# Turning the token rows of 100 expert slots: PE transposes and a PSUM copy, or pieces loaded by partition group and one VectorE transpose

## The chip, the cores and the metric

The program runs on one core of a Trainium2 chip. The core has a matmul engine (TensorE, here PE, with its weight loads listed apart as PEld), a vector engine (DVE), a scalar engine (ACT), GpSimd (POOL) and a sync engine (SP) that does no arithmetic here and issues most DMAs. Sixteen DMA engines move data between the chip's memory (HBM) and the on-chip memory (SBUF, 128 partitions). Matmul results land in PSUM. All engines run their own instruction lists in order and wait for each other through semaphores. The metric is the device time of one execution in microseconds, as the median of several.

## What is computed

Four layers are applied to 2,048 tokens of 256 channels (`x` is 2 x 1,024 x 256, all in f32). Each layer conditions the tokens, sends the result through an expert layer and adds it to `x`. Only layers 2 and 3 matter here:

```python
# layer 2, conditioning: 8 experts, two of them per token, gelu
for e in range(N_EXPERTS):
    h = jax.nn.gelu(x_flat @ r_w1[e].T, approximate=False)
    routed_out = routed_out + h @ r_w2[e].T * gates_full[:, e:e + 1]
out = (shared_out + routed_out) / (N_SHARED + TOP_K)
# layer 2, FFN: 8 experts of width 1024, two of them per token, silu-gated
g = jax.nn.silu(jnp.einsum('td,edf->etf', flat, w1_e))
u = jnp.einsum('td,edf->etf', flat, w3_e)
out_e = jnp.einsum('etf,efd->etd', g * u, w2_e)
routed = jnp.einsum('te,etd->td', gates, out_e).reshape(b, s, d)
# layer 3, conditioning: as in layer 2, with other weights
h = jax.nn.gelu(jnp.einsum('nc,ech->enh', xf, W1e), approximate=False)
y = jnp.einsum('enh,ehc->enc', h, W2e)
routed = jnp.einsum('ne,enc->nc', combine, y)
```

Beside the routed experts each of these has shared experts that all tokens pass through. Layer 3's own FFN works on another path (the class `Last`) that the change does not touch.

## The kernel before

**Slots.** Each token goes to two of eight experts. The kernel sorts these 4,096 pairs by expert into slots of 128 rows. POOL scatters each token's row into `xbuf`, an array in HBM with rows of `DR` = 258 numbers: the 256 channels, the token's row number in the result, and the token's expert. The 258 numbers are 1,032 bytes. A slot belongs to one expert, and its 128 rows are multiplied with that expert's weights. In this run layer 2's conditioning ("layer 2's MoE" below) has 35 slots, layer 2's FFN 33, and layer 3's conditioning ("layer 3's MoE") 37. Two of the FFN's 33 slots hold rows of several experts.

**One slot, step by step.** `Slots.fetch` (L1881) lets SP load the slot's 128 rows into `xs`, one row per partition, with all 258 numbers (the issue has line L418). A matmul needs the channels on the partitions, so `Slots.rows` (L1889) turns the rows: `_channel_major` (L495) does two PE transposes of 128x128 into a PSUM tile `ps_cm` (L500), and DVE copies the tile to `xsT` (L1895). Two small DVE operations (L1899, L1902) then compute `sdst`, for each row the row of `tbuf` that its result goes to; rows that do not belong to the slot get a number out of range. In the MoEs, `_gelu_products` (L1970) multiplies `xsT` with the first weight matrix (`cph`, L1976), ACT applies gelu (L1979), PE multiplies with the second matrix (`cpo`, L1983), and DVE copies the result to `ys` (L1985). In the FFN, `_ffn_products` (L1991) does this with two first matrices (`fpg`, `fpu`, L2000), a product on DVE (L2005) and ACT's copy to `ys` (L2012). `Slots.put` (L1907) lets POOL scatter `ys` to `tbuf` by `sdst` (L402).

**Order on PE.** `Series` (L1915) writes PE's order out. A call of `slot` for slot i first asks for the rows of slot i+2 (`fetch`), then puts in the transposes of slot i+1 (`turn`), the first products of slot i, the second products of slot i-1 (`close`), and so on. `stage` chains every group behind the last one with `_behind`, an order without a wait.

**Order on SP.** SP issues the row loads and, from `_expert_load` (L1857), the weight loads of each slot, in one list. A weight load is skipped on the chip when the slot's weight buffers already hold the expert. The MoEs have four sets of weight buffers, the FFN two, and later three. A weight load waits until the slot that used its set before is done. `xs` has four buffers; a row load waits until the small DVE operations of the slot four before are done. The first weights of each stage are issued before the rows. The row loads of a stage wait until all its scatters into `xbuf` have landed.

**Weight layout.** A first matrix of 256 input channels lies in SBUF as 128 partitions x 2 halves (`c`): channel `c * 128 + p` on partition `p`. A row of `xsT` holds the same channels. Each row of a MoE's matrix is 1,024 bytes, of the FFN's first two matrices 4,096.

**After the slots.** `Tokens` loads each token's two results from `tbuf` into tiles `yt` (five buffers of 128x512) and adds them up while PE does the last quarter of the shared experts.

Of the kernel before, what the change touches and what calls it, by code (L numbers as in the profile page):

```python
# [20 lines left out]
P = 128  # L21
D = 256
# [19 lines left out]
class Ring:  # L42


    def __init__(self, t, n):
        self.t, self.n, self.i, self.held = t, n, 0, set()
# [445 lines left out]
    return ps.rearrange("p c d -> p (c d)")  # L492


def _channel_major(k, psum, rows, ref=None, made=None):  # L495


    ps = psum.tile([P, 2, P], F32, name="ps_cm", tag="t", bufs=2)
    for c in range(2):
        i = k.nc.tensor.transpose(ps[:, c, :], rows[:, c * P:(c + 1) * P], k.ident)  # L500
# [24 lines left out]
def _layer0(k):  # L525
# [37 lines left out]
    with ExitStack() as ctx:  # L563
# [92 lines left out]
        shared(1, lambda f, mul, mm: rows_of(4 + f, mm))  # L656
        _layer1_loads0(k, k.pre)
        ahead(-2)
        slots = Slots(k, pool, psum, ref=sent[-1])
# [4 lines left out]
        for i in range(NS):  # L664
            if i < 18 and i % 2 == 1:
                next(mask)
            lo, cols = i * T, []
            while lo < (i + 1) * T:

                e = lo // C  # L670
                n = 64 if i % 3 == 1 else 32
                cols.append((slice(lo - i * T, lo - i * T + n), ws[e]))
                lo += n
            muls.append(split.slot(i, cols))
            next(pre, None)

            ahead(3 * (i * T // C), slots.load)
# [16 lines left out]
    def slots_over():  # L694
        k.yrows = (NS + NOV) * T
        zero = pool.tile([P, 1, DR], F32, name="l0_zero", bufs=1)
        nc.vector.memset(zero[:, :, 0:D], 0.0)
        nc.vector.memset(zero[:, :, D:], NONE)
        _zero_rows(k, ybuf[NS * T:(NS + NOV) * T, :], zero[:, :, 0:D])
        read = k.x.read  # L700
        k.x.read = k.x.read + k.x.new + [_zero_rows(k, xbuf[NS * T:, :], zero).ins.name]
        k.x.begin()
        for t in range(NT):
            k.x.scatter(k.Hr[:, t, :], rows[:, t:t + 1])
        k.ring.held = set(held)
        slots = Slots(k, pool, psum)
# [12 lines left out]
        more(0)  # L719
        k.x.read = read + k.x.read  # L720
        k.ring.i, k.ring.held = free[0], set(free[1])
# [1135 lines left out]
def _expert_load(k, eid, i, to, E, always=False):  # L1857

    nc = k.nc

    e = nc.sync.value_load(eid[0:1, i:i + 1], min_val=0, max_val=E)
    new = {} if always else {"cond": e < E}
    e = nc.s_assert_within(e, 0, E - 1, skip_runtime_bounds_check_because="at E the load is skipped")
    for t, a in to:
        nc.sync.dma_start(t, a[bass.ds(e, 1)].rearrange("o (c p) f -> p (o c) f", p=P), **new)
    return [t for t, _ in to]


# [4 lines left out]
class Slots:  # L1873

    def __init__(self, k, pool, psum, of=None, base=0, ref=None):
        self.k, self.pool, self.psum, self.of, self.base, self.ref = k, pool, psum, of, base, ref
        self.xs, self.dst = {}, {}

    def fetch(self, i):  # L1881

        if i not in self.xs:
            self.xs[i] = self.pool.tile([P, DR], F32, name="xs", bufs=4)
            self.load = self.k.x.load(self.xs[i], self.k.xbuf[i * P:(i + 1) * P, :])
            if self.ref is not None:
                _behind(self.k, self.load, self.ref)

    def rows(self, i, made=None):  # L1889
# [5 lines left out]
        turned = nc.vector.tensor_copy(xT, _channel_major(k, self.psum, xs, made=made))  # L1895
        if self.of is not None:

            n = pool.tile([P, 1], F32, name="sn", bufs=3)
            j = nc.vector.tensor_tensor(n, xs[:, D + 1:D + 2], self.of[:, i:i + 1], ALU.not_equal)  # L1899
            _behind(k, j, turned)  # L1900
            self.dst[i] = pool.tile([P, 1], U32, name="sdst", bufs=5)
            j = nc.vector.scalar_tensor_tensor(self.dst[i], xs[:, D:D + 1], -float(self.base), n,  # L1902
                                               ALU.add, ALU.add)
            _behind(k, j, turned)
        return xT

    def put(self, i, y):  # L1907
        if self.of is None:
            self.k.nc.scalar.dma_start(self.k.ybuf[i * P:(i + 1) * P, :], y)
        else:  # L1910

            self.k.t.scatter(y, self.dst.pop(i), bounds_check=2 * N - 1, oob_is_err=False)


class Series:  # L1915
# [1 line left out]

    def __init__(self, k, slots, ids):  # L1920
        self.k, self.slots, self.ids = k, slots, list(ids)
        self.xT, self.last, self.old, self.soon = {}, None, None, False
        self.fetch(0)
        self.fetch(1)
        self.turn(0)

    def stage(self, insts):

        for i in insts:
            if self.last is not None:  # L1930
                _behind(self.k, i, self.last)
        self.last = insts[-1]

    def fetch(self, n):
        if n < len(self.ids):
# [8 lines left out]
    def slot(self, i, products, weights, soon=False):  # L1944

        n = self.ids.index(i)
        self.fetch(n + 2)
        self.turn(n + 1)
        if self.soon:
            self.close()  # L1950
        self.soon = soon
        p = products(self.xT.pop(i), *weights())
        self.stage(next(p))
        self.close()
        part = next(p)
# [106 lines left out]
class Split:  # L2062
# [9 lines left out]
    def stage(self, insts):  # L2072

        for i in insts:
            if self.last is not None:
                _behind(self.k, i, self.last)
        self.last = insts[-1]

    def product(self, name, xT, cols, j):
        ps = self.psum.tile([P, self.F], F32, name=name, tag="mm")  # L2080
# [58 lines left out]
def _cond_moe(k, name, wr, bias, W1, W3, W2, nf, hold, R1, R2, gate_mult, final, lead, most, next=None):  # L2139
# [73 lines left out]
    by = Slots(k, pool, psum, of, base)  # L2213

    def slots(lo, hi):
        series = Series(k, by, range(lo, hi))
        for i in range(lo, hi):
            series.slot(i, _gelu_products(k, pool, psum), lambda: _slot_weights(k, eid, i, sets, E))
        series.close()
# [41 lines left out]
def _layer2_ffn(k):  # L2261
# [65 lines left out]
        return [_expert_load(k, mid, 3 * m + q, sets[j], E) for q, j in enumerate(to) if j is not None]  # L2327

    def slots(ids):
        series = Series(k, by, ids)  # L2330
        for n, i in enumerate(ids):
            if i == NS:
                series.slot(i, _mixed_products(k, pool, psum), lambda: mixed(0, 0, 1, 2), True)
# [562 lines left out]
```

## Time and profile before

| | |
|---|---|
| median of 8 runs | 1399.71 us (1397.0 to 1404.9) |
| profiled execution | 1401.7 us, its span 1400.0 us |
| layer 2's MoE, 438 to 511 us | PE busy 69.43 of 73.00 us, DMA share 0.67 |
| layer 2's FFN, 687 to 1035 us | PE busy 345.30 of 348.00 us, DMA share 0.55 |
| layer 3's MoE, 1162.5 to 1243 us | PE busy 75.80 of 80.50 us, DMA share 0.70 |
| PE transposes of slot rows, all layers | 258 of 273 ns (24 slots of layer 0 and the 105 of layers 2 and 3) |
| DVE copies of the turned rows | 129 of 416 ns |
| row loads issued by SP | 129 of 344 ns each, 129 KB |

How to read it: "busy" is the time in which an engine runs an instruction; matmuls overlap in PE's pipeline, so their lengths add up to more than their cost, and PE's price of an instruction is read from the start of the next. The DMA share is the mean busy share of the sixteen DMA engines. "Released by" or an arrow names what an engine waited for last. Lines of the form L1895 are lines of the kernel before.

### The profile page before, as it was taken

Reading aid. Unit: us, or ns where it says so; the run is one execution under the profiler, and the core shown is the slowest. Engines: PE = TensorE matmul, PEld = TensorE weight load, DVE = VectorE, ACT = ScalarE, POOL = GpSimd, SP = SyncE. Lnnn points to the kernel's source line nnn. Section 1 sums busy time; section 2 is a strip of 40 time slices with the busy share of each in tenths; the row PEclk is TensorE's granted clock in tenths of the full one; section 3 lists DMA queues with packets and bytes.
Section 4 is the critical chain, followed back from the end, with each engine's and each line's share of the span. In section 5 each row is a group of like instructions: output and inputs, shape, how many; then the busy total and the mean of one; then the engine's idle time right before and its main releaser. Section 6 shows DMA issues by size and latency. Waiting matters only on the chain. (4 is left out here: it accounts for less than half of the span.)

```text
span 1400.0 us, 23093 instructions
## 1 busy us (share of the span) xinstructions
PE 1360.0 (97%) x8428; PEld 955.1 (68%) x8431; DVE 460.9 (33%) x1519; ACT 302.1 (22%) x636; POOL 272.6 (19%) x308
## 2 busy tenths in 40 slices
PE   9999999999999999999999999999999999998897
PEld 4644444655657876555599999999975557875685
DVE  4523322325413444511211111111215423458432
ACT  4222221234112122211111111111112212127122
POOL 0400001300432430053000100000000073430441
PEclk9999999999999999999999999999999999999999
DMA  9979992943312852092285456266448247748670
GB/s 312 313 242 347 357 367 88 300 91 136 113 53 86 252 186 79 0 332 70 77 319 168 148 201 218 81 206 222 150 162 288 93 165 243 228 149 282 212 226 16
DMA packets 185424, 265.26 MB, mean 189 GB/s; under 512 B 16759, under 2 KB 134655, under 8 KB 185296
## 3 DMA queue, kind: packets, MB, share of 16 engines
q1 hardware_dynamic: 163984, 221.65, 48.6%
q0 software_dynamic: 13744, 36.63, 7.4%
q10 hardware_dynamic: 7568, 5.34, 1.2%
q8 instruction: 71, 1.16, 0.3%
q14 instruction: 57, 0.47, 0.1%
HBM read 283.67 MB, written 46.82 MB: 236 GB/s over the span
## 5 line engine op out<-in xcount | busy, mean ns | idle before, releaser
L402 POOL DMA_INDIRECT tbuf<-ys,sdst x105 | 103.3, 984 | 462.6 <-ACT ys L2012 301.0
L1675 PE MATMUL spo<-ring,sa 128*128 128x256 f32 x704 | 165.0, 380 | 0.6 <-DVE sa L1703 0.4
L1675 PEld LDWEIGHTS spo<-ring,sa 128*128 128x128 f32 x704 | 132.7, 190 | 46.1 <-issue 28.7
L1703 DVE TENSOR_TENSOR sa<-ssg,spu 128x512 f32<-128x512 f32 x88 | 60.3, 686 | 240.5 <-PE spu L1690 231.2
L2005 DVE TENSOR_TENSOR fa<-fsg,fpu 128x512 f32<-128x512 f32 x62 | 42.6, 687 | 278.4 <-PE fpu L2000 278.4
L2000 PE MATMUL fpg<-xsT,ring 128*128 128x128 f32 x992 | 121.1, 276 | 1.1 <-DMA ring<-in_L_w 1.1
L2000 PE MATMUL fpu<-xsT,ring 128*128 128x128 f32 x992 | 121.0, 275 | 0.6 <-DMA ring<-in_L_w 0.6
L2000 PEld LDWEIGHTS fpg<-xsT,ring 128*128 128x128 f32 x992 | 117.9, 192 | 3.6 <-issue 2.1
L2000 PEld LDWEIGHTS fpu<-xsT,ring 128*128 128x128 f32 x992 | 115.8, 192 | 0.7 <-issue 0.7
L2009 PE MATMUL fpo<-ring,fa 128*128 128x256 f32 x496 | 112.4, 380 | 0.1
L1699 ACT ACTIVATE ssg<-spg 128x512 f32<-128x512 f32 x88 | 52.5, 597 | 267.0 <-PE spg L1690 262.8
L2009 PEld LDWEIGHTS fpo<-ring,fa 128*128 128x128 f32 x496 | 92.0, 191 | 12.2 <-issue 1.1
L1690 PE MATMUL spg<-HT,ring 128*128 128x512 f32 x192 | 92.0, 594 | 3.4 <-issue 2.1
L1690 PE MATMUL spu<-HT,ring 128*128 128x512 f32 x192 | 90.2, 593 | 0.0
L1976 PE MATMUL cph<-xsT,ring 128*128 128x128 f32 x576 | 77.8, 278 | 8.2 <-DMA ring<-in_L_r 5.5
L1976 PEld LDWEIGHTS cph<-xsT,ring 128*128 128x128 f32 x576 | 70.1, 192 | 11.8 <-DVE sn L1899 5.3
L1690 PE MATMUL spg<-XT,ring 128*128 128x512 f32 x160 | 75.6, 594 | 1.2 <-PEq L2223 1.0
L1690 PE MATMUL spu<-XT,ring 128*128 128x512 f32 x160 | 75.4, 592 | 0.0
L1983 PE MATMUL cpo<-ring,ch 128*128 128x256 f32 x288 | 73.8, 380 | 0.0
L2004 ACT ACTIVATE fsg<-fpg 128x512 f32<-128x512 f32 x62 | 37.0, 597 | 143.9 <-PE fpg L2000 143.9
L1690 PEld LDWEIGHTS spu<-HT,ring 128*128 128x128 f32 x192 | 36.2, 190 | 43.9 <-issue 43.7
L1895 DVE COPY xsT<-ps_cm 128x256 f32<-128x256 f32 x129 | 53.8, 418 | 30.9 <-PE ps_cm L500 30.9
(677 smaller groups left out, 1761.5 us busy)
## 6 DMA issues: line engine op xcount, KB each, us to landing
ring<-in_L_w SPq DMA_DIRECT2D x105, 1024.0 KB
ring<-in_L_r SPq DMA_DIRECT2D x72, 512.0 KB
ring<-in_L_r SPq DMA_DIRECT2D x144, 256.0 KB
xs<-xbuf SPq DMA_DIRECT2D x129, 129.0 KB
ring<-in_L_W SPq DMA_DIRECT2D x32, 512.0 KB
yt<-tbuf SPq DMA_DIRECT2D x48, 256.0 KB
XT<-in_L_r SPq DMA_DIRECT2D x16, 512.0 KB
HT<-in_L_r SPq DMA_DIRECT2D x8, 512.0 KB
```

Of the source, the lines that this page charges most:

```text
L402: i = k.nc.gpsimd.indirect_dma_start(out=self.ap, out_offset=bass.IndirectOffsetOnAxis(ap=idx, axis=0), in_=rows, in_offset=None, **end)
L1675: mm = nc.tensor.matmul(po[g // 2][:, g % 2, :], a[:, g * P:(g + 1) * P], W2[:, f, :], start=f == 0 and g % 2 == 0, stop=f == nf - 1, skip ...
L1690: mm = nc.tensor.matmul(ps, W[:, c, f * P:(f + 1) * P], X[:, c, cols], start=c == 0, stop=c == 1)
L1699: k.silu = nc.scalar.activation(sg, pg, AF.Silu)
L1703: mul = nc.vector.tensor_mul(a, sg, pu)
L1895: turned = nc.vector.tensor_copy(xT, _channel_major(k, self.psum, xs, made=made))
L1976: made = [nc.tensor.matmul(ph[:, f, :], R1[:, c, f * P:(f + 1) * P], xT[:, c, :], start=c == 0, stop=c == 1) for f in range(2) for c in ra ...
L1983: made = [nc.tensor.matmul(po, h[:, f, :], R2[:, f, :], start=f == 0, stop=f == 1) for f in range(2)]
L2000: made = [nc.tensor.matmul(ps[:, j, :], W[:, c, (f0 + j) * P:(f0 + j + 1) * P], xT[:, c, :], start=c == 0, stop=c == 1) for ps, W in ((pg, ...
L2004: nc.scalar.activation(sg, pg, AF.Silu)
L2005: nc.vector.tensor_mul(a[:, f0:f0 + 4, :], sg, pu)
L2009: made = [nc.tensor.matmul(po, a[:, f, :], W2[:, f, :], start=f == 0, stop=f == 4 * nh - 1) for f in range(4 * nh)]
```

## The change

It concerns the slots of layers 2 and 3 (`blocks=True`); layer 0's slots are still turned by PE, but their row loads leave out the two last numbers.

- Rows are loaded in four DMAs, one for each group of 32 partitions. Partition 32q + s of the tile `xq` gets, for each block b of 32 rows, the channels 64q to 64q + 63 of row 32b + s, a run of 256 bytes. Two slots that follow each other are loaded by the same four DMAs (`plan`, at most two). The tiles share the five buffers of `yt`.
- One DVE transpose per slot (`StreamTranspose` in the instruction list) turns all 32x32 blocks. Partition 32q + r then holds the channels 64q + 2r and 64q + 2r + 1, that is channels 2p and 2p + 1 on partition p.
- The weights follow: all matrices of a slot but the last are loaded with two neighbouring rows on one partition, so that a partition's part is one run in HBM.
- The first two slots of each MoE and the first of the FFN are still loaded as whole rows and turned by PE, with every second column in each transpose.
- The row numbers and experts of all slots of a stage come in one DMA of 8-byte pieces (`numbers`), and two DVE operations compute all of `sdst` at once. They are called in the first slot after the turn of the second.
- `Series.slot` asks for the rows of slot i+3 as well.

In the instruction lists, PE has 100 pairs of transposes less in the slots that this run executes. SP's list in a MoE is: two whole-row loads, four DMAs of `xq`, the numbers, eight DMAs of `xq`, then by turns the weights of two slots and four DMAs of `xq`. On DVE the first of the two operations on the numbers (a wait for their DMA) stands after the copies of the first two turns and ahead of the third slot's transpose.

```diff
-def _channel_major(k, psum, rows, ref=None, made=None):
+def _channel_major(k, psum, rows, ref=None, made=None, pairs=False):
     ps = psum.tile([P, 2, P], F32, name="ps_cm", tag="t", bufs=2)
     for c in range(2):
-        i = k.nc.tensor.transpose(ps[:, c, :], rows[:, c * P:(c + 1) * P], k.ident)
+        i = k.nc.tensor.transpose(ps[:, c, :], rows[:, c::2] if pairs else rows[:, c * P:(c + 1) * P], k.ident)
...
-    for t, a in to:
-        nc.sync.dma_start(t, a[bass.ds(e, 1)].rearrange("o (c p) f -> p (o c) f", p=P), **new)
+    for n, (t, a) in enumerate(to):
+        form = "o (p c) f -> p (o c) f" if n + 1 < len(to) else "o (c p) f -> p (o c) f"
+        nc.sync.dma_start(t, a[bass.ds(e, 1)].rearrange(form, p=P), **new)
...
+    def plan(self, ids, rows, most):
+        ids = list(ids)
+        while ids:
+            n = 1
+            if ids[0] in rows or not self.blocks:
+                self.group[ids[0]] = None
+            else:
+                while n < most and ids[n:n + 1] == [ids[0] + n]:
+                    n += 1
+                for j in range(n):
+                    self.group[ids[j]] = ids[0], n
+            ids = ids[n:]
...
     def fetch(self, i):
-        if i not in self.xs:
-            self.xs[i] = self.pool.tile([P, DR], F32, name="xs", bufs=4)
-            self.load = self.k.x.load(self.xs[i], self.k.xbuf[i * P:(i + 1) * P, :])
...
+        if group is None:
+            self.xs[i] = self.pool.tile([P, D], F32, name="xs", bufs=4)
+            self.load(self.xs[i], k.xbuf[i * P:(i + 1) * P, 0:D])
+            return
+        lo, n = group
+        if self.of is None:
+            t = self.pool.tile([P, n, 4, 64], F32, name="xq", tag="xs", bufs=4)
+        else:
+            t = self.pool.tile([P, 2, 4, 64], F32, name="xq", tag="yt", bufs=5)
+        for q in range(4):
+            self.load(t[32 * q:32 * q + 32, 0:n].rearrange("p g b k -> p (g b) k"),
+                      k.xbuf[lo * P:(lo + n) * P, 64 * q:64 * q + 64].rearrange("(b s) k -> s b k", s=32))
...
-        turned = nc.vector.tensor_copy(xT, _channel_major(k, self.psum, xs, made=made))
-        if self.of is not None:
-            n = pool.tile([P, 1], F32, name="sn", bufs=3)
-            j = nc.vector.tensor_tensor(n, xs[:, D + 1:D + 2], self.of[:, i:i + 1], ALU.not_equal)
...
+        if self.group[i] is None:
+            self.turned = nc.vector.tensor_copy(xT, _channel_major(k, self.psum, xs, made=made, pairs=self.blocks))
+        else:
+            self.turned = nc.vector.transpose(xT.rearrange("p c (b s) -> p c b s", b=4),
+                                              xs.rearrange("p b (r c) -> p c b r", c=2))
         return xT
+
+    def numbers(self):
+        k, nc, n = self.k, self.k.nc, self.of.shape[1]
+        m = self.pool.tile([P, n, 2], F32, name="xm", tag="xs", bufs=4)
+        k.x.load(m, k.xbuf[0:n * P, D:].rearrange("(i p) d -> p i d", p=P))
+        i = nc.vector.tensor_tensor(m[:, :, 1], m[:, :, 1], self.of, ALU.not_equal)
+        _behind(k, i, self.turned)
+        self.dst = k.rp.tile([P, n], U32, name="sdst", tag="sdst")
+        nc.vector.scalar_tensor_tensor(self.dst, m[:, :, 0], -float(self.base), m[:, :, 1], ALU.add, ALU.add)
...
         self.fetch(n + 2)
         self.turn(n + 1)
+        if self.slots.of is not None and self.slots.dst is None:
+            self.slots.numbers()
...
         p = products(self.xT.pop(i), *weights())
+        self.fetch(n + 3)
...
-        series = Series(k, by, range(lo, hi))
+        series = Series(k, by, range(lo, hi), 0 if lo else 2)
...
-        series = Series(k, by, ids)
+        series = Series(k, by, ids, 1 if ids[0] == NS else 0)
```

More of the change, by code (lines that the diff above doesn't have):

```diff
@@ L658, in _layer0 @@
         ahead(-2)
-        slots = Slots(k, pool, psum, ref=sent[-1])
+        slots = Slots(k, pool, psum, ref=sent[-1], blocks=False)
+        slots.plan(range(NS), (0, 1), 1)
         split = Split(k, pool, psum, slots, F, NS)
@@ L675, in _layer0 @@
             next(pre, None)
-            ahead(3 * (i * T // C), slots.load)
+            ahead(3 * (i * T // C), slots.loaded)
         with k.tc.issue_after(split.up.ins):
@@ L705, in slots_over @@
         k.ring.held = set(held)
-        slots = Slots(k, pool, psum)
+        slots = Slots(k, pool, psum, blocks=False)
         n = nc.values_load(nov[0:1, 0:1], min_val=0, max_val=NOV)
@@ L1873, with __init__, load, rows @@
 class Slots:
-    def __init__(self, k, pool, psum, of=None, base=0, ref=None):
+    def __init__(self, k, pool, psum, of=None, base=0, ref=None, blocks=True):
         self.k, self.pool, self.psum, self.of, self.base, self.ref = k, pool, psum, of, base, ref
-        self.xs, self.dst = {}, {}
-    def fetch(self, i):
-        if i not in self.xs:
-            self.xs[i] = self.pool.tile([P, DR], F32, name="xs", bufs=4)
-            self.load = self.k.x.load(self.xs[i], self.k.xbuf[i * P:(i + 1) * P, :])
-            if self.ref is not None:
-                _behind(self.k, self.load, self.ref)
-    def rows(self, i, made=None):
+        self.xs, self.group, self.dst, self.blocks = {}, {}, None, blocks
+    def plan(self, ids, rows, most):
[10 more added lines that the diff above has]
+            ids = ids[n:]
+    def load(self, t, src):
+        self.loaded = self.k.x.load(t, src)
+        if self.ref is not None:
+            _behind(self.k, self.loaded, self.ref)
+    def fetch(self, i):
+        if i in self.xs:
+            return
+        k, group = self.k, self.group[i]
+        if group is None:
+            self.xs[i] = self.pool.tile([P, D], F32, name="xs", bufs=4)
+            self.load(self.xs[i], k.xbuf[i * P:(i + 1) * P, 0:D])
+            return
+        lo, n = group
[6 more added lines that the diff above has]
+                      k.xbuf[lo * P:(lo + n) * P, 64 * q:64 * q + 64].rearrange("(b s) k -> s b k", s=32))
+        for j in range(n):
+            self.xs[lo + j] = t[:, j]
+    def rows(self, i, made):
         k, nc, pool = self.k, self.k.nc, self.pool
@@ L1894, in rows @@
         xT = pool.tile([P, 2, P], F32, name="xsT", bufs=3)
-        turned = nc.vector.tensor_copy(xT, _channel_major(k, self.psum, xs, made=made))
-        if self.of is not None:
-            n = pool.tile([P, 1], F32, name="sn", bufs=3)
-            j = nc.vector.tensor_tensor(n, xs[:, D + 1:D + 2], self.of[:, i:i + 1], ALU.not_equal)
[L1900 to L1904, printed above, removed]
-        return xT
+        if self.group[i] is None:
[3 more added lines that the diff above has]
+                                              xs.rearrange("p b (r c) -> p c b r", c=2))
+        return xT
+    def numbers(self):
[6 more added lines that the diff above has]
+        nc.vector.scalar_tensor_tensor(self.dst, m[:, :, 0], -float(self.base), m[:, :, 1], ALU.add, ALU.add)
     def put(self, i, y):
@@ L1910, in put, with __init__ @@
         else:
-            self.k.t.scatter(y, self.dst.pop(i), bounds_check=2 * N - 1, oob_is_err=False)
+            self.k.t.scatter(y, self.dst[:, i:i + 1], bounds_check=2 * N - 1, oob_is_err=False)
 class Series:
-    def __init__(self, k, slots, ids):
+    def __init__(self, k, slots, ids, rows=0):
         self.k, self.slots, self.ids = k, slots, list(ids)
         self.xT, self.last, self.old, self.soon = {}, None, None, False
+        slots.plan(ids, self.ids[:rows], 1 if slots.of is None else 2)
         self.fetch(0)
@@ L1931, in stage @@
                 _behind(self.k, i, self.last)
-        self.last = insts[-1]
+        self.last = (insts or [self.last])[-1]
     def fetch(self, n):
@@ L2076, in stage @@
                 _behind(self.k, i, self.last)
-        self.last = insts[-1]
+        self.last = (insts or [self.last])[-1]
     def product(self, name, xT, cols, j):
```

## The prediction

> **What bounds the kernel now.** I read the page's engine totals first, then the instructions that touch the two tiles of a turn (`ps_cm`, `xsT`), then the timeline of one slot, the table by stage, and last the timeline of SP.
>
> ```profile
> span 1400.0 us, 23093 instructions
> PE 1360.0 (97%) x8428; PEld 955.1 (68%) x8431; DVE 460.9 (33%) x1519; ACT 302.1 (22%) x636; POOL 272.6 (19%) x308
> ...
> L500 PE MATMUL ps_cm<-ident,xs x258: 272/273/331, 78.4 to 1238.7; 128*128 128x128 f32 x129
> L1895 DVE COPY xsT<-ps_cm x129: 412/416/425, 78.9 to 1239.2; 128x256 f32<-128x256 f32 x129
> ```
>
> PE is busy nearly all the time, so what PE no longer does can count. But 273 ns is the pipelined length of one transpose, not its price. The price stands in the order of time, here in layer 2's FFN (matmul starts, then lengths):
>
> ```profile
> 806.61 0.38 PE L500 MATMUL ps_cm<-ident,xs 128*128 128x128 f32 x2
> 806.83 1.95 PE L2000 MATMUL fpg<-xsT,ring 128*128 128x128 f32 x16
> ```
>
> Both transposes move the next matmul by 806.83 - 806.61 = 0.22 us. The same 0.22 us stands in the small slots (443.98 to 444.19, 445.95 to 446.17). A small slot is 445.95 - 443.98 = 1.97 us of PE.
>
> The table by stage (span, PE busy, weight loads, DVE, ACT, POOL, clock, DMA share, GB/s) shows where PE is not the only limit. 438 to 511 are the 35 slots of layer 2's MoE, 687 to 1035 the 33 of its FFN, 1162.5 to 1243 the 37 of layer 3's MoE:
>
> ```profile
> 460.00:475.00 15.00, 14.33 (x101) 12.89 (x100) 7.38 (x29) 2.68 (x7) 6.88 (x7) 1.00 0.92 290
> 725.00:800.00 75.00, 75.00 (x572) 72.25 (x571) 13.01 (x35) 10.96 (x21) 6.88 (x7) 1.00 0.53 179
> 1170.00:1185.00 15.00, 13.80 (x93) 12.02 (x92) 6.70 (x26) 2.61 (x7) 6.36 (x7) 1.00 0.98 312
> 1200.00:1215.00 15.00, 12.76 (x87) 11.07 (x85) 6.32 (x25) 2.30 (x6) 5.90 (x6) 1.00 1.00 329
> 1215.00:1230.00 15.00, 15.00 (x109) 13.94 (x108) 8.18 (x32) 2.68 (x7) 7.26 (x8) 1.00 0.51 143
> ```
>
> In the FFN, PE is full and the DMA engines half idle. In the MoEs there are stretches at 0.92 to 1.00 DMA share in which PE loses 0.7 to 2.2 us of 15: the slots that bring new expert weights. In the issue times of SP the weight DMAs that are skipped last 73 ns and the real ones 372 ns, so the two kinds can be counted: of the 31 weight pairs issued between the slots of layer 2's MoE 14 are real, of the 33 in layer 3's 17.
>
> In such a stretch SP has no time left either:
>
> ```profile
> 461.31 0.41 SPq L418 DMA_DIRECT2D xs<-xbuf  x1
> 462.04 1.14 SPq L1865 DMA_DIRECT2D ring<-in_L_r  x2
> 463.28 0.41 SPq L418 DMA_DIRECT2D xs<-xbuf  x1
> 464.01 1.14 SPq L1865 DMA_DIRECT2D ring<-in_L_r  x2
> 465.25 0.41 SPq L418 DMA_DIRECT2D xs<-xbuf  x1
> ```
>
> One row load and two weight loads take SP 463.28 - 461.31 = 1.97 us, the same as PE's slot.
>
> **The change, part by part.**
>
> *PE's turns go.* The lists of instructions show 100 of the 105 slots of layers 2 and 3 without transposes (33 + 32 + 35). At 0.22 us that is 22.0 us of PE, the upper end of what the change can bring.
>
> *DVE turns instead.* The copy from PSUM (416 ns) and two one-column operations (149 to 220 ns and 159 ns) become one transpose of 128x256 f32. No row of this trace is a DVE transpose. From below: the cheapest DVE row, 0.15 us. From above: the 128x512 f32 product, 0.69 us, if it walks its input twice. I take the 128x256 copies, 0.42 us, the same count of elements per partition. In a small slot DVE then does 0.42 + 0.43 (the copy to `ys`) = 0.85 of about 1.76 us, so up to 1.3 us per turn it is hidden by PE; the cover is gone above that. Matmuls no longer wait for a PSUM round trip but for the rows' DMA directly. Rows are issued up to three slots ahead, one more than before, so this costs nothing.
>
> The Trainium skill, "VectorE: DVE Perf Modes", The three transpose paths, gives 311 ns for a 128x128 bf16 transpose on VectorE, in 32x32 blocks only, and 390 ns on TensorE. By these, two halves would make 0.62 us, which is still hidden, so the sum would not move.
>
> *Rows in 256-byte pieces.* The trace also keeps every DMA packet's size and time. Medians: 8 B 9 ns, 256 B 18 ns, 512 B 32 ns, 1,024 B 46 ns, 1,032 B 47 ns, 2,048 B 84 ns. A slot's rows were 128 packets of 1,032 B, 8 on each of 16 engines: 0.38 us. They become 512 packets of 256 B, 32 on each: 0.58 us at 18 ns. The 128 packets of that size were contiguous ones, so 18 ns is the low end; the 512 B price (32 ns, 1.02 us) is the high end. I take 18 ns, the row of the same size. The first weight matrix goes from 256 rows of 1,024 B to 128 of 2,048 B: 16 x 46 = 0.74 us to 8 x 84 = 0.67 us. A slot with new weights thus costs 0.20 - 0.07 = 0.13 us more of all engines.
>
> The Trainium skill, "DMA: Bandwidth & Descriptors", Specifications, speaks against this edit: a transfer wants at least 512 B for line rate. Its section Why small descriptors are slow puts the overhead at 256 B at 27%; on a quarter of the 1,024 B row that would be 14.6 ns and 0.47 us per slot, less than the sum takes.
>
> *SP issues more.* Two slots now take four row DMAs instead of two. At 0.37 us of issue (the rows with 256 pieces) and 0.05 us between them that is 4 x 0.42 = 1.68 us per pair. A slot's two weight loads take SP 1.46 us when real (461.72 to 463.18 above) and 0.91 us when skipped (445.72 to 446.63, two of 73 ns and their register work). Per slot: 0.84 + 0.91 = 1.75 us skipped, 0.84 + 1.46 = 2.3 us real. PE's new slot is 1.97 - 0.22 = 1.75 us. So SP becomes the pace-setter of the MoE slots: level with PE and without slack where weights are skipped, 0.3 us slower than before where they are real, less a lead of two to three slots. In the FFN a slot lasts some 10.5 us and SP idles; queues of POOL and ACT issue what they did.
>
> *The row numbers.* One DMA per stage brings 39 x 128 (41 x 128 in the FFN) pieces of 8 B, at 312 per engine x 9 ns = 2.8 us. It is queued on SP behind the two (one) whole-row loads and one group of four; on DVE its comparison stands ahead of the third slot's turn, so a late landing holds DVE, and with it PE's third slot. In layer 3's MoE SP's first row load goes out late:
>
> ```profile
> 1160.47 4.40 SPq L418 DMA_DIRECT2D xs<-xbuf  x6
> ...
> 1162.59 0.20 PEld L500 LDWEIGHTS ps_cm<-ident,xs 128*128 128x128 f32 x2 [0.54 <-DMA xs<-xbuf]
> ```
>
> A row load lands 2.1 us after its issue. The numbers go out at 1160.47 + 2 x 0.4 + 4 x 0.42 = 1162.9 and land at 1162.9 + 2.1 + 2.8 = 1167.8; with 0.2 us for the comparison and 0.42 us for the turn PE's third slot starts at 1168.4. PE would reach it at about 1166.3 (two first products and one second). Stall: about 2 us; low end 0, high end 14 us at the 1,024 B price (312 x 46 ns). In layer 2's MoE the first row load goes out at 429.37 and PE arrives at 437.85; the same chain ends before PE's third slot: 0 to 1 us. In the FFN it goes out at 662.41 for 686: nothing. The 105 pairs of small DVE operations and DVE's waits for `sdst` (14.5 us in all) were beside PE: nothing. The five slots that PE still turns read every second column; at worst that doubles 0.22 us, 1.1 us in all; nothing taken. The FFN's first two weight matrices come in longer runs, at half-idle DMA engines: nothing.
>
> **Sum.** FFN: 32 x 0.22 = 7.0, less 0.4 for two slots in the weight-bound stretch after 700 (DMA share 0.97): -6.6. MoEs, slots without new weights: 33 - 14 = 19 in layer 2 and 35 - 17 = 18 in layer 3, of which four lie between two loaded runs and only let SP catch up: 33 at 0.17 (0.22 less a quarter, as SP has no slack): -5.6. The slots with new weights: between -0.22 each, had PE alone the say, and +0.3 each by SP; by the DMA engines +0.13. For 31 I take +0.05, because SP's and the rows' lead cover part: +1.6. Start of layer 3's MoE +2.0, of layer 2's +0.5. Total -8.1 us. The profiled execution took 1401.7 us (span 1400.0), so 1393.6; it lies 2.0 above the median of the eight runs, 1399.7, against which I say 1391.6, rounded 1392.
>
> **Rivals.**
> 1. *Everything is covered* (SP's lead and the half-idle DMA engines of the skipped slots carry the loaded ones): -22 + 3 = -19, about 1381. For it: shares of 0.67 and 0.70 over the whole MoE stages. Against: 0.98 to 1.00 in the stretches.
> 2. *The MoEs give nothing*: SP's 2.3 us in 31 slots and the starts eat their gain; only FFN's 6.6 minus some 5 remain: 1398. For it: SP's pace above.
> 3. *Slower: 256 B pieces out of rows of 1,032 B cost as 512 B ones.* Then 31 loaded slots need 1.02 - 0.38 - 0.07 = 0.57 us more of saturated engines, +17.7, against -6.6 and -5.6 and with +2.5 at the starts: +8, 1408. It decides from about 24 ns a packet, where 31 x 0.31 = 9.7 meets the gains less the starts.
> 4. *Slower: the turn itself.* Above 1.97 - 0.43 = 1.54 us a turn, DVE sets a longer slot than PE did; at 2.0 us it is 70 x 0.46 = 32 us, less FFN's 6.6: 1425. Nothing in the trace is that slow per element.
>
> That the turns stay on PE is excluded by the instruction lists.
>
> **How the numbers follow.** Forecast (1387 to 1396) 0.46; rival 1 0.16; rival 2 0.16; rival 3, and the numbers' load at its high end, 0.16; rival 4 0.06. One part in five of rival 2 still falls under -0.2% (2.8 us, about what a measurement of this kernel can tell from no change). So faster 0.65, same 0.13, slower 0.22. The range, 1382 to 1406, leaves out half of rival 1, rival 4 and the upper part of rival 3, together under 0.2; the forecast's own range is 1387 to 1396.
>
> **What would show it.** Right: `ps_cm<-ident,xs` 29 instead of 129 pairs; FFN slots 0.22 us shorter with PE still full; DVE rows of a 128x256 transpose near 0.42 us; the MoEs' slots at 1.75 to 1.8 us in skipped stretches and no faster in loaded ones; an idle of some 2 us on PE at the third slot of layer 3's MoE, laid to the row numbers. Wrong: a turn over 1.3 us, packets of 256 B over 24 ns, PE idle in the FFN, or SP never waiting in the skipped stretches.

## The result: slower, by 0.35%

The changed kernel took 1404.14 us (median of 12 runs, 1401.6 to 1409.85); the kernel before, run beside it, 1400.06 us (median of 35). The ratio is 1.0035, with a 95% interval of 1.0025 to 1.0045. The forecast was 1392 and faster. The profiled execution took 1403.56 us, with a span of 1401.8 against 1400.0.

The page of the changed kernel (totals, then one of the costliest groups: busy, mean ns, idle before it and who ended it), and the view of the tile of pieces `xq` (durations: least, median, most):

```profile
span 1401.8 us, 22601 instructions
PE 1343.7 (96%) x8228; PEld 936.5 (67%) x8231; DVE 440.0 (31%) x1315; ACT 302.4 (22%) x636; POOL 272.7 (19%) x308
...
L2018 PE MATMUL cph<-xsT,ring 128*128 128x128 f32 x576 | 80.0, 284 | 26.3 <-DMA ring<-in_L_r 15.3
```

```profile
L418 SPq DMA_DIRECT2D xq<-xbuf x208: 302/449/3064, 431.0 to 1237.8; - x104
L1931 DVE STREAM_TRANSPOSE xsT<-xq x100: 404/438/448, 440.0 to 1240.1; 128x256 f32<-128x256 f32 x100
```

PE has 16.3 us less of busy time, and the turn on DVE takes 0.438 us. But the first product of the MoEs' slots (`cph`) now stands idle for 26.3 us, most of it for weights (`ring<-in_L_r`). The same group on the page of before had 8.2 us:

```profile
L1976 PE MATMUL cph<-xsT,ring 128*128 128x128 f32 x576 | 77.8, 278 | 8.2 <-DMA ring<-in_L_r 5.5
```

The matmul starts and the copies to `ys` put the loss in its places:

| us | before | after |
|---|---|---|
| layer 2's MoE, first to last result tile | 70.4 | 72.8 |
| layer 2's FFN, first to last `fpg` | 344.6 | 338.2 |
| end of the FFN to the last result tile of layer 3's MoE | 198.9 | 205.1 |
| all the rest | 786.1 | 785.7 |

The FFN gained 6.4 us; the MoEs lost 2.4 and 6.2. With the 0.4 us less in the rest, that sums to the 1.8 us between the two spans.

The FFN now, in the order of time (start, length): nothing stands between the products any more, and each group of 16 starts 1.78 us after the one before.

```profile
807.65 1.95 PE L2042 MATMUL fpg<-xsT,ring 128*128 128x128 f32 x16
809.43 1.95 PE L2042 MATMUL fpu<-xsT,ring 128*128 128x128 f32 x16
811.22 3.62 PE L2051 MATMUL fpo<-ring,fa 128*128 128x256 f32 x16
```

The table by stage after (span, PE busy, weight loads, DVE, ACT, POOL, clock, DMA share, GB/s), the same stretches as in the prediction:

```profile
460.00:475.00 15.00, 12.12 (x71) 10.68 (x70) 5.03 (x12) 1.99 (x6) 5.34 (x7) 0.89 0.99 264
...
1170.00:1185.00 15.00, 10.48 (x64) 8.25 (x62) 4.37 (x11) 2.28 (x6) 4.98 (x6) 1.00 1.10 284
1200.00:1215.00 15.00, 10.82 (x60) 9.09 (x59) 4.26 (x10) 1.92 (x5) 4.78 (x5) 0.89 1.03 273
1215.00:1230.00 15.00, 12.91 (x88) 11.48 (x87) 5.67 (x14) 2.69 (x7) 6.89 (x7) 1.00 0.66 173
```

In the first three PE loses 3 to 4.5 us of 15 where it lost 0.7 to 2.2, and the DMA engines are as busy as before while they move less: 264, 284 and 273 GB/s for 290, 312 and 329. Both SP and the DMA engines are suspects. SP in the first of these stretches:

```profile
460.08 2.02 SPq L418 DMA_DIRECT2D xq<-xbuf  x4
462.42 3.03 SPq L1867 DMA_DIRECT2D ring<-in_L_r  x4
465.54 1.89 SPq L418 DMA_DIRECT2D xq<-xbuf  x4
467.76 3.09 SPq L1867 DMA_DIRECT2D ring<-in_L_r  x4
470.95 0.41 SPq L418 DMA_DIRECT2D xq<-xbuf  x1
```

A pair of slots takes SP 465.54 - 460.08 = 5.46 and then 5.41 us: 2.7 us a slot, where the kernel before took 1.97. A third cost shows on PE there (start, length, idle before):

```profile
462.00 1.13 PE L2018 MATMUL cph<-xsT,ring 128*128 128x128 f32 x8
462.96 1.03 PE L2025 MATMUL cpo<-ring,ch 128*128 128x256 f32 x4
466.78 1.95 PE L2018 MATMUL cph<-xsT,ring 128*128 128x128 f32 x8 [2.79 <-DMA ring<-in_L_r]
468.52 1.91 PE L2025 MATMUL cpo<-ring,ch 128*128 128x256 f32 x4
470.23 1.10 PE L2018 MATMUL cph<-xsT,ring 128*128 128x128 f32 x8
```

After 2.79 us without work the next products run at half speed, 1.95 and 1.91 us for the 1.13 and 1.03 above. By their starts the two take 3.45 us (466.78 to 470.23) instead of some 1.76, so a wait of 2.8 us costs about 4.5. The granted clock of the stretch is 0.89; before it was 1.00 in all of these.

Last, the start of layer 3's MoE:

```profile
1158.48 0.45 SPq L418 DMA_DIRECT2D xm<-xbuf  x1
...
1158.98 6.41 SPq L418 DMA_DIRECT2D xq<-xbuf  x8
...
1163.68 0.20 DVE L1940 TENSOR_TENSOR xm<-xm,l3c_of 128x39 f32<-128x39 f32 x1 [4.47 <-DMA xm<-xbuf]
...
1164.36 1.16 PE L2018 MATMUL cph<-xsT,ring 128*128 128x128 f32 x8 [2.75 <-DVE xsT L1931]
```

The row numbers (`xm`) land 5.2 us after their issue, DVE waits 4.47 us for them and PE 2.75 us behind DVE.

### The profile page after: what moved, and what is told of

Same layout as the page of the kernel before. It is cut to its first block, busy times and chain, and to the rows that moved or that the text cites. A ratio compares the mean times of both kernels' runs of the same rounds, so it can differ in the third digit from the quotient of the medians.

```text
span 1401.8 us, 22601 instructions
## 1 busy us (share of the span) xinstructions
PE 1343.7 (96%) x8228; PEld 936.5 (67%) x8231; DVE 440.0 (31%) x1315; ACT 302.4 (22%) x636; POOL 272.7 (19%) x308
## 5 line engine op out<-in xcount | busy, mean ns | idle before, releaser
L2018 PE MATMUL cph<-xsT,ring 128*128 128x128 f32 x576 | 80.0, 284 | 26.3 <-DMA ring<-in_L_r 15.3
L2018 PEld LDWEIGHTS cph<-xsT,ring 128*128 128x128 f32 x576 | 76.0, 197 | 37.4 <-issue 23.2
L2025 PE MATMUL cpo<-ring,ch 128*128 128x256 f32 x288 | 76.4, 390 | 0.0
L2021 ACT ACTIVATE ch<-cph 128x256 f32<-128x256 f32 x72 | 27.7, 384 | 130.9 <-PE cph L2018 130.8
```

Of the source, the lines that this page charges most:

```text
L2018: made = [nc.tensor.matmul(ph[:, f, :], R1[:, c, f * P:(f + 1) * P], xT[:, c, :], start=c == 0, stop=c == 1) for f in range(2) for c in ra ...
L2025: made = [nc.tensor.matmul(po, h[:, f, :], R2[:, f, :], start=f == 0, stop=f == 1) for f in range(2)]
```

## The experiments

Two theories for the slots with new weights. **S**: SP, at 2.7 us a slot, sets the pace. **D**: the DMA engines do; worked out from the packets' mean times in 460 to 475, a slot's weights and rows took (512 x 51 + 128 x 57) / 16 ns = 2.09 us of all engines before and (256 x 51 + 128 x 112 + 512 x 23) / 16 = 2.45 us after. (Shares of 1.10 and 1.03 show that packets' times overlap, so these are upper estimates.) Each ratio is to the kernel before run beside it. The runs were spread over several chips; on most the kernel before took 1400.4 to 1400.6 us, on one 1417.66 (kernels marked *), and there only ratios and the inner stages compare. The stage columns come from one profiled execution each. Columns in us: layer 2's MoE, FFN and FFN's end to the last result tile of layer 3's MoE as above, and in that MoE first to last result tile.

| kernel | median us | ratio, 95% | L2 MoE | FFN | to end of L3 MoE | L3 tiles |
|---|---|---|---|---|---|---|
| before | 1400.06 | 1 | 70.4 | 344.6 | 198.9 | 76.6 |
| after | 1404.14 | 1.0035 (1.0025 to 1.0045) | 72.8 | 338.2 | 205.1 | 80.2 |
| e4_ffn_only | 1393.98 | 0.9954 (0.9938 to 0.9970) | 70.8 | 338.1 | 196.0 | 74.8 |
| e5_moe_only | 1412.10 | 1.0078 (1.0062 to 1.0095) | 73.3 | 345.5 | 205.2 | 79.4 |
| e1_act4 | 1402.16 | 1.0006 (0.9994 to 1.0018) | 71.9 | 338.1 | 202.7 | 76.4 |
| e1_act2 | 1397.99 | 0.9983 (0.9972 to 0.9994) | 69.0 | 337.9 | 205.0 | 76.3 |
| e2_half_l3 | 1404.08 | 1.0025 (1.0014 to 1.0035) | 74.7 | 338.3 | 202.6 | 77.9 |
| e10_act2_half_l3 * | 1418.29 | 1.0000 (0.9983 to 1.0017) | 70.1 | 338.1 | 214.0 | 69.3 |
| e7_rows | 1391.35 | 0.9939 (0.9919 to 0.9959) | 68.3 | 337.9 | 195.4 | 73.3 |
| e9_rows_split * | 1435.12 | 1.0129 (1.0107 to 1.0151) | 79.5 | 338.1 | 220.4 | 85.5 |
| e11_near * | 1410.55 | 0.9951 (0.9933 to 0.9969) | 70.9 | 338.0 | 209.7 | 74.4 |
| e3_late | 1406.63 | 1.0030 (1.0016 to 1.0044) | 75.1 | 337.9 | 205.4 | 78.0 |
| e3_no_num_l3 | 1402.62 | 1.0015 (1.0002 to 1.0027) | 73.3 | 338.2 | 202.1 | 80.1 |
| e12_parts | 1393.21 | 0.9946 (0.9932 to 0.9960) | 69.1 | 337.9 | 197.7 | 76.6 |

The same code of layer 2's MoE (after, e2, e3_no_num_l3) gives 72.8 to 74.7 us, so a stage tells differences from about 2 us on. The stretch to the end of layer 3's MoE is coarser: before and e4, in which that MoE is the same, have 198.9 and 196.0.

### One part alone

e4: in both MoEs `blocks=False` for their `Slots`, rows of `DR` columns with two small DVE operations per slot, the old weight layout. e5: the same for the FFN instead.

```diff
-    by = Slots(k, pool, psum, of, base)
+    by = Slots(k, pool, psum, of, base, blocks=False)
...
-    return _expert_load(k, eid, i, sets[i % len(sets)], E, i < len(sets))
+    return _expert_load(k, eid, i, sets[i % len(sets)], E, i < len(sets), False)
```

> Only the FFN of layer 2 has its rows in four pieces and turned by DVE, with the new layout of its first weight matrix and the row numbers in one load. Both MoEs are as in the kernel before: whole rows with their numbers, turned by PE, old weight layout. If the parts add, the FFN keeps the 6.4 us that the two traces show for it and nothing else changes: 1393 to 1394.5, faster than both. Rival: the FFN's gain comes from something that the MoE before it left (weights already there, the clock), then half of it or less: 1397 or more.

> The reverse: both MoEs as changed, the FFN as in the kernel before. If the parts add, the FFN's 6.4 us are missing and the MoEs' loss stands alone: 1409 to 1412, 9 to 11 us slower than the kernel before. If the MoEs' loss is in part the FFN's doing, less: 1403 to 1407.

Both came as expected, 1393.98 and 1412.10 (a hair over its 1412). The parts add within the spread of the runs: -0.46% and +0.78% make +0.32%, against +0.35% for both.

### SP or the DMA engines

Row DMAs on ACT's queue, from the fifth slot of a MoE on (e1_act4: all four of a pair; e1_act2: two):

```diff
     def load(self, dst, src, by=None):
-        i = self.k.nc.sync.dma_start(dst, src)
+        i = (by or self.k.nc.sync).dma_start(dst, src)
...
+                      k.nc.scalar if self.base != 4096 and self.of is not None and lo >= 4 and q >= 2 else None)
```

> In both MoEs the four row DMAs of every pair of slots from the fifth slot on are issued by ACT instead of SP; the packets, their sizes and their number stay. Theory S (SP's issues set the pace of the slots with new weights): in the stretches where slots bring weights, SP took 0.98 us of row issues and 1.6 us of weight issues per slot (pairs at 460.08, 465.54, 470.95), against PE's 1.76. Without the row issues SP is at 1.6 and the slots go back towards 1.76: the excess over 1.76 is 11 us in layer 2's MoE and 11 in layer 3's beside its late start, so 10 to 18 us go and the time is 1386 to 1394. ACT then has 0.38 us of gelu and 0.98 of issues per slot, so it does not take SP's place. Theory D (the DMA engines' time for the 256 B packets sets it: share 0.99 in 460 to 475): nothing changes, 1402 to 1405. Both at work: a part, 1396 to 1401.

At 1402.16 e1_act4 looked like D. But ACT had a cost of its own; its order of time in 458 to 476:

```profile
460.57 4.54 ACTq L418 DMA_DIRECT2D xq<-xbuf  x4
465.21 0.91 ACT L2022 ACTIVATE ch<-cph 128x256 f32<-128x256 f32 x2 [4.36 <-DMA xq<-xbuf]
467.29 3.03 ACTq L418 DMA_DIRECT2D xq<-xbuf  x4
```

The gelu for slots already multiplied stood 4.36 us behind row DMAs. So the result did not decide, and the next runs were made to.

> In both MoEs two of the four row DMAs of a pair are issued by ACT, two by SP (with all four on ACT: 1402.16 us, ACT's gelu stood up to 4.4 us behind its own issues, which took 0.75 to 1.1 us each in the stretches with weights). Theory D: all issues wait for the same engines, whoever makes them: 1401 to 1404. Theory S, with the gain of four on ACT lost to gelus held up: SP has 0.49 + 1.6 = 2.1 us per slot with weights against 2.6 and ACT half the hold-up, so the excess over 1.76 us is cut by more than half, 1393 to 1398.

1397.99 is at the upper edge of what S gave: 0.5% under the changed kernel, with every packet still there. SP's own waits agree. Added up over 458 to 512 us they were 14.2 us in the kernel before, 3.7 in the changed one, where SP hardly ever waits, and 11.3 in e1_act2. And its layer 3 had a handicap. Ahead of that MoE, ACT held its own silu behind a row load that waits for the rows' scatter, and PE waited with it (waits of ACT, then of PE, in 1120 to 1172 of e1_act2):

```profile
ACT ssg L1700 <- DMA xbuf<-Xt,l3c_rows: 13.6, 1, 13.6
```

```profile
PE spo L1676 <- DVE sa L1704: 3.6, 1, 3.6
```

The same waits stand in e1_act4 (13.5 and 3.4 us). The reverse relief, half the packets with as many DMAs on SP:

```diff
+            m = 1 if self.base == 0 and self.of is not None else n
-            self.load(t[32 * q:32 * q + 32, 0:n].rearrange("p g b k -> p (g b) k"),
+            self.load(t[32 * q:32 * q + 32, 0:m].rearrange("p g b k -> p (g b) k"),
...
-            self.xs[lo + j] = t[:, j]
+            self.xs[lo + j] = t[:, j % m]
```

> Only in layer 3's MoE, each of the four row DMAs of a pair loads the rows of the first slot alone, and both slots are computed from them: half the 256 B packets, as many DMAs on SP, as many turns. It leaves out the row loads of every second slot, and those slots' results are not the reference's. All up to layer 3's MoE is the changed kernel. From the end of the FFN's matmuls to the last result tile of layer 3's MoE it took 198.9 us before, 205.1 after. Theory D (the DMA engines' time for 256 B packets paces the slots with weights): a slot's 512 packets took 512 x 23 ns / 16 = 0.74 us of all engines in 460 to 475; half of it gone on some 17 slots with weights is 6.3 us: 199 us for the stretch, 1397 to 1399 in all. Theory S (SP's issues): the number of issues is the same, only the shorter issue of a smaller DMA (0.34 for 128 pieces against 0.45 for 256) gives up to 0.2 us per slot, 0 to 3.4 us: 202 to 205 us for the stretch, 1401 to 1404 in all.

1404.08: no time back that can be told (1.0025 against 1.0035, overlapping intervals), and 202.6 us for the stretch, where S put it and D did not. The issue got hardly shorter, though (a median of 0.43 us for 0.45, not 0.34), so the 2.5 us by which the stretch is under 205.1, if they are more than the spread of single executions, are the packets' and not SP's. The table by stage and SP of this kernel:

```profile
1170.00:1185.00 15.00, 11.05 (x62) 9.60 (x63) 4.35 (x10) 1.92 (x5) 5.14 (x6) 0.89 0.85 256
...
1200.00:1215.00 15.00, 11.79 (x76) 9.83 (x74) 4.94 (x12) 2.59 (x7) 6.54 (x7) 1.00 0.83 236
```

```profile
1201.62 2.58 SPq L1867 DMA_DIRECT2D ring<-in_L_r  x4
1204.30 1.89 SPq L418 DMA_DIRECT2D xq<-xbuf  x4
1206.51 2.88 SPq L1867 DMA_DIRECT2D ring<-in_L_r  x4
1209.49 2.95 SPq L418 DMA_DIRECT2D xq<-xbuf  x4
```

The DMA share fell from 1.10 and 1.03 to 0.85 and 0.83, and PE still lost 3 to 4 us of 15, since SP needs 1209.49 - 1204.30 = 5.2 us a pair, much as in the changed kernel.

Could full DMA engines be what makes SP's issues long? In the changed kernel the issue of a piece DMA had a median of 0.449 us both in 438 to 459, where the DMA share is 0.52, and in 460 to 475, where it is 0.99. So it is as long either way.

Then both reliefs at once:

> Both reliefs at once in layer 3's MoE: two of a pair's four row DMAs on ACT (in both MoEs), and in layer 3's MoE the rows of the first slot of a pair alone loaded and used for both (half the 256 B packets; every second slot's results are not the reference's). From the first to the last result tile of layer 3's MoE: 80.2 us changed, 77.9 with half the packets alone, 76.3 with ACT's help alone; 62.5 would be 36 slots at PE's pace with none held up. If SP's issues come first and the DMA engines' time right behind, each relief alone shows only the gap between the two and both together more than the sum (2.3 + 3.9 = 6.2): under 73 us, 1391 to 1395 in all. If only SP's issues count: 75 to 77 us, 1396 to 1398.

69.3 us for layer 3's tiles, under the 73 named (layer 2's MoE, where both kernels are the same, took 70.1 on this chip and 69.0 in e1_act2): 10.9 us off, where each alone gave 2.3 and 3.9. But part of this is a head start. PE came to the stage some 20 us later (first result tile 144.7 us after the FFN's end, 124.8 in the changed kernel), and SP had issued its opening run of row loads by 1180.3 us, before PE's first product at 1185.1; in the changed kernel PE began at 1158.7 and SP ended that run at 1165.4. Far from the start, from result tile 17 to 24, the stage took 21.4 us changed, 18.5 with half the packets, 18.1 with ACT's help and 16.2 with both. So both together go further than either, and the DMA engines do hold slots once SP is relieved; but there it is 5.2 us against 2.9 and 3.3, not more than the sum, and up to 1.7 us of each is a spell of half clock (below) that only the changed kernel has in these tiles. "More than the sum" is not shown. The forecast of the total failed: ACT held the silu 14.4 us there and PE waited 9.3 us for it before the stage, which ate the gain.

### SP's issues without pieces or a turn

e7: all rows of the MoEs whole, by one DMA a slot, turned by PE; layout and numbers stay as changed.

```diff
-        series = Series(k, by, range(lo, hi), 0 if lo else 2)
+        series = Series(k, by, range(lo, hi), hi - lo)
```

> In both MoEs rows come whole (128 packets of 1,024 B, one DMA per slot) and PE turns them, as before; the weights' new layout (2,048 B packets) and the numbers in one load stay. The FFN is the changed one. Only the pieces with DVE's turn are undone. With MoEs as before altogether the time was 1393.98 us. If the pieces are the whole loss of the MoEs: 1393 to 1395. If the numbers' load costs layer 3's start 2.5 to 4 us as well, 1396 to 1398. If the 2,048 B packets (112 ns in 460 to 475 where two of 1,024 B took 102) cost: 128 x 10 / 16 = 0.08 us on each of 31 slots, 2.5 us more.

1391.35, lower than any expectation, and the fastest of all. Its stages and SP:

```profile
460.00:475.00 15.00, 15.00 (x108) 14.27 (x108) 5.72 (x16) 2.93 (x8) 7.61 (x8) 1.00 0.98 310
```

```profile
462.17 0.47 SPq L418 DMA_DIRECT2D xs<-xbuf  x1
462.96 1.10 SPq L1867 DMA_DIRECT2D ring<-in_L_r  x2
464.15 0.48 SPq L418 DMA_DIRECT2D xs<-xbuf  x1
464.96 1.10 SPq L1867 DMA_DIRECT2D ring<-in_L_r  x2
466.15 0.52 SPq L418 DMA_DIRECT2D xs<-xbuf  x1
```

SP is at 2.0 us a slot, PE at 1.99, and PE loses nothing in this stretch although the DMA share is 0.98 (it loses 1.4 us of 15 in 475 to 490, and 0.6 and 0.45 in 1170 to 1185 and 1185 to 1200). e9 adds one thing to this kernel, a second row DMA per slot:

```diff
-            self.load(self.xs[i], k.xbuf[i * P:(i + 1) * P, 0:D])
+            m = 2 if self.blocks and self.base != 4096 and i >= 2 else 1
+            for h in range(m):
+                self.load(self.xs[i][h * P // m:(h + 1) * P // m],
+                          k.xbuf[i * P + h * P // m:i * P + (h + 1) * P // m, 0:D])
```

> The version with whole rows turned by PE in both MoEs (1391.35 us), but each slot's rows from the third slot on are loaded by two DMAs of 64 rows each instead of one of 128: as many packets of the same size, one issue more per slot on SP. So a slot has two row DMAs, as many as with the pieces, and nothing else of the change. Theory S (SP's issues): SP goes from 1.6 + 0.4 to some 2.4 us per slot with weights against PE's 1.98 and falls behind as with the pieces; on 31 such slots 0.4 us each, less the lead: 5 to 12 us more, 1396 to 1403, and the slots with weights wait for them. Theory D (the DMA engines' time): packets are the same, 1391 to 1393.

```profile
466.20 1.10 SPq L418 DMA_DIRECT2D xs<-xbuf  x2
467.64 1.10 SPq L1867 DMA_DIRECT2D ring<-in_L_r  x2
468.84 1.18 SPq L418 DMA_DIRECT2D xs<-xbuf  x2
470.35 1.10 SPq L1867 DMA_DIRECT2D ring<-in_L_r  x2
471.55 0.45 SPq L418 DMA_DIRECT2D xs<-xbuf  x1
```

```profile
460.00:475.00 15.00, 12.13 (x83) 11.12 (x82) 4.54 (x12) 1.92 (x5) 5.66 (x7) 1.00 0.76 214
```

1.0129 / 0.9939 = 1.019: 27 us for some 70 more issues, with the same packets. S, and more than the 5 to 12 us it gave, since two DMAs of 64 rows took SP 1.1 us where one of 128 took 0.41 to 0.52. SP's slot is 471.55 - 468.84 = 2.7 us, that of the changed kernel; PE loses 2.9 us of 15 while the DMA engines are at 0.76 (0.68 to 0.93 in five other stretches of the two MoEs, and PE loses 1.7 to 3.7 there). SP's waits in 458 to 512 add up to 2.8 us. So more issues on SP alone, without pieces and without a turn on DVE, make a loss of this kind, and a larger one: to the same e7 the changed kernel loses some 13 us.

The Trainium skill, "DMA: Bandwidth & Descriptors", Issuing engines are not separate DMA queues, says that issuing from several engines only saves sequencer time, and that this time is usually small beside the transfer. e1_act2 agrees that such time is saved; that nothing else is saved no run shows. And here that time is not small: a slot's issues, with their register work, gaps and SP's short waits, take 2.7 us and its packets 2.45.

e11 adds the new weight layout to e4 (`near`, and PE turning `rows[:, c:D:2]`):

> The version with only the FFN changed (1393.98 us), and in addition both MoEs get the weights' new layout (first matrix in 2,048 B packets, PE turning even and odd channels apart); rows whole with their numbers per slot. With the numbers in one load as well it was 1391.35 us. It parts the 2.6 us between them. If the layout is worth it (PE waited 0.9 us less for weights, and 128 descriptors go for 256): 1391 to 1392. If it is the two small DVE operations per slot that are gone (PE's matmul stood 1.9 us behind them in layer 2's MoE): 1393 to 1395.

0.9951 against e4's 0.9954, with e4's times for layer 2's MoE, the FFN and layer 3's tiles: the layout gives nothing that can be told. Under load a packet of 2,048 B took 112 ns, two of 1,024 B 102. What e7 has beyond e4 is then the row numbers in one load, which take two small DVE operations out of each slot (PE stood 1.9 us behind `sn` in e4's layer 2). But by its edit e7 also asks for the rows of slot i+3, which e4 and e11 do not, and loads 1,024 bytes a row for 1,032; the three were not parted. The intervals of e4 and e7 overlap, so the 2.6 us between them are not certain.

### The row numbers

e3_late loads them from ACT and puts DVE's wait three slots later, keeping three result tiles back; e3_no_num_l3 leaves the load out in layer 3; e12 is e7 with the load in three.

```diff
-        k.x.load(m, k.xbuf[0:n * P, D:].rearrange("(i p) d -> p i d", p=P))
+        i = k.nc.scalar.dma_start(self.xm, k.xbuf[0:n * P, D:].rearrange("(i p) d -> p i d", p=P))
...
+            if n == 3:
+                self.slots.numbers()
```

> The DMA of the row numbers goes out on ACT's queue instead of SP's, and DVE's two operations on them stand ahead of the fourth slot instead of ahead of the third's turn; the first three result tiles are kept until then and are scattered together. If the wait for the numbers costs what the profile shows in layer 3's MoE (PE idle 2.8 to 3.2 us behind DVE's turn, SP's next row DMA held 2.95 us behind the 8 B pieces), 2.5 to 4 us go and the time is 1400 to 1401.5. Rival: the 4,974 packets of 8 B keep all DMA queues busy from 1160 to 1163, rows and first weights come late whatever waits for the numbers, and at most 1 us goes: 1403 to 1405.

> Only in layer 3's MoE, the row numbers are not loaded: DVE makes some from a table that is on the chip, and the results of that stage go to rows that are not theirs; its scatters have the size they had. This leaves out the load of the numbers and the wait for it. When ACT loaded the numbers and the wait was put later, the stretch from the end of the FFN to layer 3's last result tile was 205.4 us against 205.1, so the wait was not it. Rival that is left: the 4,974 packets of 8 B hold the DMA engines for 3 us at the start, rows and first weights come that much late whoever issues the numbers: 2.5 to 4 us go, 201 to 202.5 us for the stretch, 1400 to 1401.5 in all. If the numbers cost nothing in either way: 204 to 206 us, 1403 to 1405.

> The version with whole rows turned by PE in both MoEs (ratio to the kernel before 0.9939), with the row numbers of a MoE in three loads instead of one: those of slots 0 to 7 in the first slot, of 8 to 23 in the second, of the rest in the fourth; each part is compared by DVE up to two slots after its load goes out, and the packets are as many. If the 8 B packets at the start cost layer 3's MoE what leaving them out gave (3.0 us between the end of the FFN and the last result tile), the part of it that only stands ahead of the first rows and weights comes back: 1 to 2.5 us, ratio 0.992 to 0.9935. Rival: the packets cost the same wherever they stand, since the DMA engines are full through that stage (0.92 to 0.99 in 1153 to 1185), and two more issues on SP: ratio 0.9935 to 0.995.

e3_late gained nothing, but it is no clean test: ACT again stood 13.8 us ahead of its silu before layer 3, and PE 3.8 us behind that. e3_no_num_l3 puts the price of the load and its wait at 202.1 against 205.1 us, 3.0 us, which is about the spread of this stretch, and at 0.2% in all (1402.62, a little over the expected 1401.5; the intervals just touch). e12 gained nothing either, as its rival said: 197.7 us where e7 had 195.4. Whether any order of these packets is free was not settled.

## Why the prediction was wrong

- **FFN, -6.6**: -6.4. Right.
- **The turn, 0.42 us, hidden**: 0.438 and hidden. Right; rival 4 falls.
- **256 B packets, 18 ns**: 18 ns is their median over the whole run, but 23 ns their mean in the loaded stretches, and packets of 2,048 B took 112 ns there for the 84 taken. So a slot with weights costs the DMA engines 0.36 us more, not 0.13. Rival 3 named these packets, and its sum, 1408, lies nearest; but as the only cause it falls with e2, and its closeness is luck.
- **Slots without new weights, -5.6**: they run at 1.76 us for 1.98, 0.22 each. There are 38 of them (see below), which is -8.4. Right, and a little low.
- **Start of layer 3's MoE, +2.0**: 3.0 by e3_no_num_l3, with as much spread. Right in kind; whether it is the wait or the 8 B packets themselves stays open. Layer 2's +0.5 was not measured apart.
- **31 slots with new weights, +0.05 each, +1.6**: this step failed. (There are 30: in layer 2's MoE of the kernel before SP issues 13 real pairs, five from 459.8, four from 472.7 and four from 494.5 us on, not 14.) Measured: layer 2's MoE lost 2.4 us although 20 slots gained 0.22, so its 13 loaded slots lost 6.8, 0.52 each; layer 3's lost 6.2, less 3.0 for the start, and 18 slots gained, so its 17 lost 7.2, 0.42 each. Together 14.0 us instead of 1.6. With the other terms: -6.4 - 8.4 + 14.0 + 3.0 = 2.2, less 0.4 in the rest of the span: 1.8, the difference of the spans. (It must come out, since the 14.0 is what the other terms leave.) The ratio of the medians says some 5 us; single executions leave that much open.

The step had the mechanism, SP falling behind, with the bounds -0.22 and +0.3, and two things were wrong in it. The price: SP's sum said 2.3 us a slot, the trace has 2.7, 0.49 instead of 0.42 us for a DMA of pieces with its gap (4 x 0.49 = 1.97 of the 5.43 us a pair) and so 1.73 instead of 1.46 for a slot's weights with SP's short waits among them. And the discount from +0.3 to +0.05 for a lead of two to three slots. Take the skipped slots at 1.98 or 1.76 us and the last at 0.86 out of each stage: the loaded slots then took on average 2.31 us (layer 2) and 2.36 (layer 3) before, 2.83 and 2.81 after. That is SP's 2.7 and a little more, so no lead shows. A likely reason, not tested: the loaded slots come in runs (five pairs of real weight loads in a row from 459.8 to 469.6 us in the kernel before), and a lead pays for a run once, not for each slot in it. The same figures show that the 1.97 us of the kernel before, from which the step reckoned, was already 2.3 on average. At +0.3 the sum would have been -0.4, no change; with the measured 14.0 in place of 1.6 it is +4.3, slower.

One cost was not in the sum at all, the clock. The changed kernel's trace has three spells of half clock in its MoEs, each 3.41 us long, from 466.89, 504.44 and 1211.00 us. They start whole multiples of 3.41 us apart (11 and 207). In the 3.41 us ahead of each, PE had been busy for 0.62, 0.89 and 1.55 us. An idle of 2.75 us from 1161.61 on, nearly as long as the 2.79 above, drew none: it lies across two steps of that grid, with 1.81 and 2.26 us of work in them. So the length of the idle alone does not decide here. The Trainium skill, "TensorE: Matmul & The Clock Gate", What's actually happening, has PE's clock at half after an idle window of about 3.4 us that is free-running, and back after as long a busy one. The trace agrees on the length and the fixed grid; but the windows ahead of the three spells were not wholly idle.

A spell costs at most 1.7 us, so at most 5.1 of the 14.0. It is not needed for the loss: e9, which lost more, has none in its MoEs, and neither has e7, where all stretches of the MoEs have a granted clock of 1.00.

## What to carry to other kernels

Count the issuing engine's time per step as one counts an engine's: so many DMAs by their issue from a row of the same shape, with register work and gaps, and compare it with the step, not with the transfer. Where two resources stand some 10% apart (here SP at 2.7 us and the DMA engines at 2.45, with PE at 1.76), relieving one may show little but the other; relieve both, and compare where the start of the stage plays no part. A change that gains where there is slack and loses where there is none is best made only in the first: here in the FFN, not in the MoEs, 0.9954 (e4) instead of 1.0035, or 0.9939 (e7) with the row numbers in one load as well.

## Of the hardware, not expected

- The issue of a piece DMA took a median of 0.449 us on SP and 0.310 us on ACT (view of the tile `xq` in e1_act2):

```profile
L418 SPq DMA_DIRECT2D xq<-xbuf x142: 303/449/3933, 430.9 to 1232.3; - x142
...
L418 ACTq DMA_DIRECT2D xq<-xbuf x66: 309/310/469, 430.2 to 1229.5; - x66
```

- Two row DMAs of 64 rows (0.45 and 0.60 us in e9, some 1.1 together) take SP over twice what one of 128 rows takes (0.41 to 0.52 in e7).
- A DMA moved to another engine's queue takes its waits along: a row load that waits for a scatter held ACT for 13.5 (e1_act4) and 13.6 us (e1_act2), and a row load in e10 for 14.4, with ACT's silu behind it.
- Half clock came in spells of 3.41 us on a fixed grid: after steps with 0.62, 0.89 and 1.55 us of work, not after steps with 1.81 and 2.26 us.
